# Layer norm rows on ScalarE, a layer norm's statistics six steps ahead, and one tile of the output projection in another step

## The chip, the core and the metric

The kernel runs on one core of a Trainium2 chip. Its engines work side by side: TensorE (PE, with its weight loads listed as PEld), VectorE (DVE), ScalarE (ACT), GpSimd (POOL) and SyncE (SP), which here only issues DMAs. The metric is the device time of one execution, in microseconds (us); a time given for a kernel is the median of its runs.

## The reference

The input has 16 elements of 512 rows by 128 (float32). For each element:

```python
h = layernorm(x) * (1 + ca) + sa
x = x + ga * attention(h)          # causal, 16 heads of 64, output projection W_out + b_out
h = layernorm(x) * (1 + cb) + sb
x = x + gb * moe(h)                # 8 experts 128 -> 512 -> 128, gelu, softmax over the top 2
```

The six modulation rows sa, ca, ga, sb, cb, gb are `silu(c) @ wmod`, one set for each element, and the two gates are kept at least 0.25 away from zero.

## The kernel before

**Attention, the first four fifths.** A loop runs over 128 pairs (b, n): element b from 0 to 15, and n from 0 to 7 for a pair of heads. One turn, by `attend`, is called a step here, and step n is the turn with that n. A step does, in PE's order: the scores of this pair (`scores`, L470, three banks for query tiles 3, 2 and 1+0), the product with V of the pair before (`z`, L558), the q and k projections of the next pair (`project_qk`, L426), the step's "units" (other PE work), and the transposes of this pair's probabilities (`transposes`, L530: tile 3, then 2, then 1 and 0).

The work between scores and transposes is a chain over four engines, once for each query tile: DVE takes the masked row maximum (`masked_max`, L487), ACT the exponentials (`exps`, L503), DVE a reciprocal of the row sum (`divide`, L510), POOL the division (L116, as all of POOL's operations that go through a helper). Then PE transposes, and the tile is copied to `pT`: tiles 3, 1 and 0 by DVE, tile 2 by ACT (L540). ACT also evicts z, q/k, v and hT.

All PSUM tiles come from one ring of four tiles of two banks. A tile can be written when the tile four places earlier has been evicted, so a late eviction holds up a matmul group later on.

**What sets the order.** PE, DVE, ACT and SP run exactly in program order, and POOL's operations are pinned to theirs. Other work is put into the steps by a table, `BESIDE`, and its variant `BESIDE_LAST` for element 15. Its slots are places in `attend`: `quiet` (a POOL scatter that waits for the first maximum), `a` (after the divide of tile 2), `b` (after that of tile 1), `units` (PE work, ahead of the transposes), `c` (ahead of the transposes and pT copies on DVE), `last` (behind them). A word `s.` stands for the next element's first layer norm and projections (`starting`), `f.` for the element before's output projection, residual, second layer norm and gate logits (`finishing`), `r.` for the routing two elements back, `1` for one scatter DMA of routed rows. The table before:

```python
0: dict(a="r.share", b="r.choose", quiet="1", units="f.o0 r.count", c="1 s.ln0 f.add0 r.rank", last="f.x0"),
1: dict(quiet="1", units="f.o1", c="1 s.ln1 r.extend r.place f.add1", last="s.dev f.x1"),
2: dict(b="s.norm0", quiet="1", units="v0", c="s.norm1 r.pick", last="rows"),
3: dict(units="s.hT", c="f.ln0"),
4: dict(quiet="1", units="v1", c="f.ln1 r.carry", last="f.dev"),
5: dict(a="f.off", quiet="1", units="s.v0", c="f.norm"),
6: dict(quiet="1", units="s.v1 f.hT", last="f.store"),
7: dict(units="f.lg", c="f.wt", last="m.mods"),
```

The names that matter:
- `ln0`, `ln1` (`layernorm`, L342, L343, L345): mean and variance of half an element's rows on DVE; `dev`: the power -0.5 on POOL; `norm0`, `norm1` (`normalise`, L354): (x - mean) * rstd on DVE, two row tiles each; `off` (`offset`, L389): -mean * rstd, used by the second layer norm, which POOL applies.
- `o0`, `o1` (`project_out`): two of the four row tiles of the output projection each; `add0`, `add1` (`projected`, L639): bias and eviction on DVE; `x0`, `x1` (`attended`): gate and residual on POOL.
- `extend`, `place`, `pick`, `carry`: parts of the routing on DVE, which give each routed row its slot; `pick` (L892 to L898) also takes the two expert weights.
- `lay_out`: fills DRAM, once, at the end of step 1 of element 0: `wall` (the experts' weights in rows, L274 to L284), `hs` (10 MB of empty rows, L288) and `ys` (L293). All go through SP's queue.
- `load_x` (L137): loads an element's rows, also on SP. It is issued at the start of step 0 of element b for element b + 1; only x_0 and x_1 are loaded at the start of the kernel.

**The experts, the last fifth.** The routed rows were scattered to slots in DRAM (`hs`); tiles of 256 rows go through one expert each (L1027 to L1065), are scattered back, and combined (`combine`, L1154 to L1163).

Of the kernel before, what the change touches and what calls it, by code (L numbers as in the profile page):

```python
# [9 lines left out]
FP = mybir.dt.float32  # L10
I32 = mybir.dt.int32
AF = mybir.ActivationFunctionType
# [3 lines left out]
P = 128  # L16
# [5 lines left out]
def kernel(  # L22
# [65 lines left out]
    def bank(name):  # L88
        return banks(name)[:, 0, :]
# [45 lines left out]
    def load_x(b):  # L135
        x = work.tile([P, NT, D], FP, tag="x", name=f"x_{b}", bufs=3)
        nc.sync.dma_start(out=x, in_=resid[b].rearrange("(t p) d -> p t d", p=P))  # L137
        x_tiles[b] = x
# [133 lines left out]

    def lay_out():
        nc.sync.dma_start(out=wall[:, :HID], in_=w1.rearrange("e d h -> (e d) h"))  # L274
        for k in range(NHC):
            nc.sync.dma_start(
                out=wall[:, HID + k * D : HID + (k + 1) * D].rearrange("(e p) d -> e p d", p=P),
                in_=w2[:, k * P : (k + 1) * P, :],
            )
        nc.sync.dma_start(  # L280
            out=wall[:, HID + NHC * D : HID + NHC * D + D].rearrange("(e p) d -> e p d", p=P),
            in_=b2.unsqueeze(1).to_broadcast([E, P, D]),
        )
        nc.sync.dma_start(  # L284
            out=wall[:, ROWW - NHC :].rearrange("(e p) k -> p e k", p=P),
            in_=b1T.rearrange("p (e k) -> p e k", k=NHC),
        )
        nc.sync.dma_start(  # L288
            out=hs.rearrange("(s p c) d -> p s (c d)", p=P, c=C),
            in_=empty.rearrange("p c d -> p (c d)").unsqueeze(1).to_broadcast([P, NST, C * (D + 1)]),  # L290
        )

        nc.sync.dma_start(  # L293
            out=ys[2 * LATE * S :, :].rearrange("(s p) d -> p s d", p=P),
            in_=empty[:, 0, :D].unsqueeze(1).to_broadcast([P, 2 * (B - LATE) * NT, D]),
        )
# [53 lines left out]

    def normalise(b, which, half_of):
        xn, mv, rstd = xn_tiles[b, which]
        for t in range(2 * half_of, 2 * half_of + 2):
            nc.vector.tensor_scalar(  # L354
                xn[:, t, :], x_tiles[b][:, t, :], mv[:, t, 0:1], rstd[:, t : t + 1], ALU.subtract, ALU.mult
            )
# [28 lines left out]

    def offset(b):
        _, mv, rstd = xn_tiles[b, 1]
        offs[b] = small.tile([P, NT], FP, tag="off", name=f"off_{b}", bufs=2)
        nc.vector.scalar_tensor_tensor(offs[b], mv[:, :, 0], -1.0, rstd, ALU.mult, ALU.mult)  # L389

    def second_norm(b):
# [3 lines left out]
        row = mods[b][:, 2 * D :]  # L395
        off = offs.pop(b)
        for t in range(NT):
# [149 lines left out]
    def z(b, n, ps=None):  # L547
# [6 lines left out]
        for t in reversed(range(NT)):  # L554
            for own in (True, False)[: NT - t]:
                cols = slice(t * P, (t + 1) * P) if own else slice((t + 1) * P, S)
                for j in range(2):
# [6 lines left out]
                    )  # L564
        zT = work.tile([P, S], FP, tag="zT", name=f"zT_{b}_{n}", bufs=NP + 2)
        zT_tiles[b, n] = zT
# [54 lines left out]

    def project_out(b, half_of):
        ps = bank(f"ps_o_{b}_{half_of}")
        attn_out[b, half_of] = ps
        for t in range(2 * half_of, 2 * half_of + 2):
            for n in range(NP):
                in_columns(
                    ps[:, ts(t % 2, D)],
                    zT_tiles[b, n][:, ts(t, P)],
                    wo_sb[:, n, :],  # L630
                    start=(n == 0),
                    stop=(n == NP - 1),
                )

    def projected(b, half_of):
        if half_of == 0:
            attn_sum[b] = work.tile([P, NT, D], FP, tag="o", name=f"o_{b}", bufs=1)
        ps = attn_out.pop((b, half_of))
        nc.vector.tensor_tensor(  # L639
            attn_sum[b][:, 2 * half_of : 2 * half_of + 2, :],  # L640
            ps[:, : 2 * D].rearrange("p (t d) -> p t d", d=D),
            bo_sb.unsqueeze(1).to_broadcast([P, 2, D]),
            ALU.add,
        )
# [88 lines left out]
    def starting(b):  # L733
# [5 lines left out]
            dev=(deviation, 0),  # L739
            norm0=(normalise, 0, 0),  # L740
            norm1=(normalise, 0, 1),
            hT=(first_hT,),
# [4 lines left out]
    def finishing(b):  # L747
# [4 lines left out]
            o0=(project_out, 0),  # L752
            o1=(project_out, 1),
            add0=(projected, 0),
            add1=(projected, 1),
            x0=(attended, 0),
            x1=(attended, 1),
            ln0=(layernorm, 1, 0),
            ln1=(layernorm, 1, 1),
            dev=(deviation, 1),  # L760
            off=(offset,),
            norm=(second_norm,),
# [36 lines left out]
    def route(b):  # L799
# [87 lines left out]
        def pick():  # L887
            wt, _ = chosen_by.pop(b)
            chosen = tiles["chosen"]
# [5 lines left out]
            slots_of[b] = tmp("slot", [P, 2, NT], I32, bufs=2)  # L895
            nc.vector.tensor_copy(slots_of[b], where)
            nc.vector.tensor_tensor(part, chosen, wt.unsqueeze(1).to_broadcast(both), ALU.mult)
            nc.vector.tensor_reduce(weight[:, :, at], part, AX.X, ALU.add)  # L898
# [9 lines left out]
        def experts():  # L908
# [23 lines left out]
        parts = dict(  # L932
            choose=choose, count=count, rank=rank, extend=extend, place=place, pick=pick, carry=carry_on
        )
# [204 lines left out]
    def fetch_x(b):  # L1139
        x2[b] = work.tile([P, NT, D], FP, tag="zT", name=f"x2_{b}", bufs=NP + 2)  # L1140
        nc.sync.dma_start(out=x2[b], in_=kept(x_rows[b]))
        load_gate_b(b)

    def combine(b, width=NT):

        x, got = x2.pop(b), got_tiles.pop(b)
        gb = gates_b.pop(b)
        y = work.tile([P, NT, D], FP, tag="zT", name=f"y_{b}", bufs=NP + 2)
        results[b] = y
# [97 lines left out]
    def dense_rest(b):  # L1247

        h = work.tile([P, NT, D], FP, tag="hT1", name=f"rest_h_{b}")
        nc.sync.dma_start(out=h, in_=kept(h2_rows[b]))  # L1250
        x = work.tile([P, NT, D], FP, tag="x", name=f"rest_x_{b}", bufs=3)
        load = nc.sync.dma_start(out=x, in_=in_rows(out[b]))
# [24 lines left out]
    warm_up(5)  # L1277
    begin["norm0"]()
    copied_scT()
    begin["norm1"]()  # L1280
    modulation()
# [5 lines left out]
    for task in later:  # L1287
# [4 lines left out]
    BESIDE = {  # L1292
        0: dict(a="r.share", b="r.choose", quiet="1", units="f.o0 r.count", c="1 s.ln0 f.add0 r.rank",
                last="f.x0"),
        1: dict(quiet="1", units="f.o1", c="1 s.ln1 r.extend r.place f.add1", last="s.dev f.x1"),
        2: dict(b="s.norm0", quiet="1", units="v0", c="s.norm1 r.pick", last="rows"),
        3: dict(units="s.hT", c="f.ln0"),
        4: dict(quiet="1", units="v1", c="f.ln1 r.carry", last="f.dev"),
        5: dict(a="f.off", quiet="1", units="s.v0", c="f.norm"),
        6: dict(quiet="1", units="s.v1 f.hT", last="f.store"),  # L1300
        7: dict(units="f.lg", c="f.wt", last="m.mods"),
    }

    BESIDE_LAST = {
        0: dict(a="r.share", b="r.choose", quiet="1", units="f.o0 r.count", c="1 f.add0 r.rank", last="f.x0"),
        1: dict(quiet="1", units="f.o1", c="1 r.extend r.place f.add1", last="f.x1"),
        2: dict(quiet="1", units="v0", c="r.pick", last="rows"),
        3: dict(quiet="1", units="v1", c="1 f.ln0 r.carry", last="r.experts"),
        4: dict(quiet="1", c="1 f.ln1", last="f.dev"),
        5: dict(a="f.off", quiet="1", c="1 f.norm"),  # L1310
        6: dict(quiet="1", units="f.hT", c="1", last="f.store"),
        7: dict(units="f.lg o01234", c="f.wt", late="o56", last="m.mods"),
    }

    FIRST = {
        0: dict(
            units=[begin["v0"], begin["v1"], modulation_matmuls],
            c=[modulation_rows],
            last=[lambda: later.pop()(), load_rest],
        ),  # L1320
        1: dict(units=[transposed_b1], c=[copied_b1], last=[lay_out]),
    }
    ends = finishing(LAST)
    for at, (b, n) in enumerate(pairs):
        prev = pairs[at - 1] if at else None
        nxt = pairs[at + 1] if at + 1 < len(pairs) else None
        if n == 0 and b + 1 < B and b + 1 not in x_tiles:
            load_x(b + 1)
        if n == 7 and b < LAST:
            routes[b - 1] = route(b - 1) if b else {}  # L1330
        known = {
            "s": starting(b + 1) if b + 1 < B else {},
            "f": finishing(b - 1) if b else {},
            "r": routes.get(b - 2, {}) | ({"share": finishing(b - 2)["share"]} if b > 1 else {}),
# [3 lines left out]
        for where, words in (BESIDE if b < LAST else BESIDE_LAST)[n].items():  # L1338
            for word in words.split():
# [8 lines left out]
                else:  # L1348
                    of, name = word.split(".")
                    tasks = [known[of][name]] if name in known[of] else []  # L1350
                beside.setdefault(where, []).extend(tasks)
        attend((b, n), prev, nxt, beside)

# [41 lines left out]
    steps = {at: [ends[name] for name in names] for at, names in steps.items()}  # L1395
    for at, name in enumerate(("share", "choose", "count", "rank", "extend", "place", "pick", "carry")):
        steps.setdefault(1 + at, []).append(routes[LATE][name])
# [95 lines left out]
```

## Time and profile before

| | us |
|---|---|
| median of the runs | 1549.77 (1549.37 to 1551.87, 3 runs) |
| the profiled execution | 1549.97 |
| its span, first to last instruction | 1548.2 |
| first scores matmul of element 0, 1, 2, 3 | 13.0, 86.3, 171.0, 248.6 |
| first scores matmul of element 6 and 7 | 481.93, 559.75 |
| first scores matmul of element 15, first expert matmul | 1182.6, 1269.7 |
| last PE instruction | 1528.2 |

The profile is of one execution. A line of a timeline has start and length in us, engine, source line, operation, output<-inputs, shape, count, and in brackets the idle time before it with what ended it. A line of the windows has a stretch, its length, and the busy time of PE, PEld, DVE, ACT and POOL in it (with counts), then PE's granted clock, the DMA share and GB/s. Each matmul and weight load stands twice in the counts, and a busy PE need not be PE at its best: a group that waits between two matmuls can show as one long busy piece.

### The profile page before, as it was taken

How to read it: one execution, taken by the hardware profiler on the slowest of the kernel's cores; microseconds unless marked ns; L12 is line 12 of the kernel's file. 1: busy time of each engine (PE TensorE's matmuls, PEld its weight loads, DVE VectorE, ACT ScalarE, POOL GpSimd, SP SyncE). 2: the span in 40 equal slices, each digit the busy share in tenths (PEclk: the TensorE clock that was granted, in tenths of full speed). 3: DMA queues.
4: the chain of work that ended last, by engine and by line, in shares of the span. 5: the costliest groups of instructions: out<-in, count | busy, mean ns of one | idle time of the engine just before them, and what ended most of it. 6: DMA issues, size and time to landing. Idle time of an engine off the chain costs nothing. (4 is left out here: it accounts for less than half of the span.)

```text
span 1548.2 us, 45464 instructions
## 1 busy us (share of the span) xinstructions
PE 1509.1 (97%) x16798; PEld 1048.2 (68%) x16798; DVE 1094.1 (71%) x4258; ACT 1062.6 (69%) x2887; POOL 966.7 (62%) x1561
## 2 busy tenths in 40 slices
PE   9989999999999999999999999999999999999994
PEld 5565757575756565656565656666666679999994
DVE  6657787878787878787878787878787844443444
ACT  6857777778777777777777777777777754444543
POOL 5435566666666666666666666666666656667663
PEclk9999999999999999999999999999999999999997
DMA  4860101010101010101010101010100047799994
GB/s 127 219 169 9 36 13 38 20 38 20 38 21 36 22 36 22 36 22 36 22 36 22 36 22 36 23 36 22 36 22 29 28 139 245 242 346 317 306 307 147
DMA packets 97902, 130.80 MB, mean 84 GB/s; under 512 B 10776, under 2 KB 73165, under 8 KB 97673
## 3 DMA queue, kind: packets, MB, share of 16 engines
q1 hardware_dynamic: 86745, 102.16, 21.5%
q0 software_dynamic: 10608, 24.73, 4.6%
q8 instruction: 136, 2.23, 0.6%
q14 instruction: 93, 0.76, 0.2%
q10 hardware_dynamic: 320, 0.93, 0.2%
HBM read 86.95 MB, written 46.07 MB: 86 GB/s over the span
## 5 line engine op out<-in xcount | busy, mean ns | idle before, releaser
L503 ACT ACTIVATE p<-p,nmax 128x512 f32<-128x512 f32 (+3 forms) x1024 | 560.3, 549 | 216.5 <-DVE nmax L487 214.9
L116 POOL TENSOR_SCALAR p<-p,rden 128x512 f32<-128x512 f32 (+3 forms) x1024 | 525.6, 529 | 230.0 <-DVE rden L510 225.0
L487 DVE CUSTOM_DVE_ANT_0 p<-sc,mask 128x512 f32<-128x512 f32 (+3 forms) x1024 | 439.9, 486 | 9.6 <-PE sc L470 9.0
L540 DVE COPY pT<-ps_pT 128x1024 f32<-128x1024 f32 (+2 forms) x384 | 276.6, 771 | 83.7 <-PE ps_pT L530 82.0
L470 PE MATMUL sc<-qk 64*128 64x512 f32 (+3 forms) x2048 | 311.0, 441 | 6.1 <-DVE o L639 4.4
L558 PE MATMUL ps_z<-pT,v 128*64 128x128 f32 x3556 | 304.0, 322 | 0.0
L116 POOL DMA_INDIRECT hs<-rows,slot x128 | 134.3, 1049 | 216.0 <-DVE nmax L487 144.8
L470 PEld LDWEIGHTS sc<-qk 64*128 64x128 f32 x2048 | 185.3, 189 | 117.0 <-DVE pT L540 55.8
L558 PEld LDWEIGHTS ps_z<-pT,v 128*64 128x64 f32 x3556 | 200.8, 137 | 33.7 <-issue 0.2
L530 PEld LDWEIGHTS ps_pT<-ident,p 64*128 64x128 f32 x5120 | 177.4, 139 | 62.9 <-POOL p L116 55.9
L530 PE MATMUL ps_pT<-ident,p 64*128 64x64 f32 x5120 | 201.3, 226 | 9.5 <-POOL p L116 6.6
L1043 ACT ACTIVATE hid<-ps_h,wexp 128x256 f32<-128x256 f32 x272 | 106.5, 474 | 127.9 <-issue 126.6
L503 ACT ACTIVATION_READ_ACCUMULATOR p<-p,nmax 128x1 f32 x1024 | 191.4, 187 | 0.0
L510 DVE RECIPROCAL rden<-den 128x2 f32<-128x2 f32 x512 | 84.0, 164 | 147.8 <-ACT p L503 143.2
L116 POOL DMA_INDIRECT ys<-yrow,to_rows x136 | 136.1, 1001 | 56.6 <-issue 31.0
L540 ACT COPY pT<-ps_pT 128x768 f32<-128x768 f32 x128 | 102.0, 797 | 98.6 <-PE ps_pT L530 95.9
L1056 PE MATMUL ps_e<-wexp,hid 128*128 128x128 f32 x1088 | 132.4, 275 | 0.0
L426 PE MATMUL ps_qk<-hT,wq_sb 128*64 128x512 f32 x508 | 130.6, 592 | 0.0
L426 PE MATMUL ps_qk<-hT,wk_sb 128*64 128x512 f32 x508 | 130.6, 592 | 0.0
L1041 PE MATMUL ps_h<-hsT,wexp 128*128 128x256 f32 x544 | 129.5, 381 | 0.9 <-DVE hsT L1029 0.9
L434 ACT COPY qk<-ps_qk 128x1024 f32<-128x1024 f32 x127 | 127.6, 1004 | 0.0
L1056 PEld LDWEIGHTS ps_e<-wexp,hid 128*128 128x128 f32 x1088 | 126.8, 192 | 0.1
(146 smaller groups left out, 1505.9 us busy)
## 6 DMA issues: line engine op xcount, KB each, us to landing
wexp<-wall SPq DMA_DIRECT2D x68, 578.0 KB
hs<-empty SPq DMA_DIRECT2D x1, 10062.0 KB
hrow<-hs SPq DMA_DIRECT2D x68, 129.0 KB
rows<-h_rows SPq DMA_DIRECT2D x32, 256.0 KB
got<-ys POOLq DMA_DIRECT2D x15, 512.0 KB, 6.3
x<-in_L_attn_resid_dram SPq DMA_DIRECT2D x16, 256.0 KB
mods<-mods_rows SPq DMA_DIRECT2D x16, 256.0 KB
x_rows<-x SPq DMA_DIRECT2D x16, 256.0 KB
```

The source lines that it names most:

```text
L116: made = getattr(nc.gpsimd, name)(*args, **kw)
L426: nc.tensor.matmul(out[r], lhsT[:, r], rhs, **flags)
L434: evictions.append(lambda: nc.scalar.copy(qk, ps))
L470: nc.tensor.matmul(ps[:, j, off : off + w], qk[r, 0, ts(i, P)], qk[r, 1, :w], start=True, stop=True)
L487: masked = nc.vector.tensor_tensor_reduce(out=p[:, j, r], in0=ps[:, j, r], in1=mask[:, S - (i + 1) * P : S], scale=-QSCALE, scalar=-MASKED ...
L503: nc.scalar.activation(p[:, j, r], p[:, j, r], AF.Exp, bias=nmax[:, j : j + 1], scale=-1.0, accum_out=den[:, j : j + 1])
L530: nc.tensor.transpose(ps[:, h, off + 2 * t + j, :], p[rows, j, at + t * P : at + (t + 1) * P], ident[rows, rows],)
L540: engine_copy(pT[:, : 2 * (i + 1), ts(i, P)].rearrange("p k (h q) -> p k h q", h=2), ps[:, :, off : off + 2 * (i + 1), :].rearrange("p h k ...
L558: nc.tensor.matmul(ps[j * DH : (j + 1) * DH, cols], v[:, t, col + j * DH : col + (j + 1) * DH], pT[:, t, j, cols], start=(t == NT - 1), st ...
L1041: nc.tensor.matmul(parts[j], wts[:, ts(j, P)], hT, start=True, stop=True)
L1043: nc.scalar.activation(hid[:, j, :], parts[j], AF.Gelu, bias=wts[:, ROWW - NHC + j : ROWW - NHC + j + 1])
L1056: nc.tensor.matmul(ps[:, ts(c, D)], hid[:, j, ts(c, P)], wts[:, HID + j * D : HID + (j + 1) * D], start=(j == 0), stop=(j == NHC - 1),)
```

## The change

It makes these edits:

- `normalise` goes from DVE to ACT: four `activation` calls an element (`Identity`, scale rstd, bias -mean * rstd), at the end of step 1 (`s.norm`). The bias comes from `offset`, which the first layer norm now uses too (`s.off` in step 0).
- The statistics (`t.ln0`, `t.ln1`, `t.dev`) of element b + 2 are taken in steps 5 and 6 of element b, where those of b + 1 were taken in steps 0 and 1. Element 1's are taken in element 0's first two steps as before. x has four buffers instead of three, and is loaded at the start of step 4 for element b + 2.
- `extend` and `place` move from slot `c` of step 1 to slot `b` of steps 1 and 2. The weights leave `pick` as a part of their own, `weigh`, in step 6.
- The output projection is cut in three: tiles 0 and 1 in step 0, tile 2 in step 1, tile 3 in step 3 (`o2`, `add2`); `x1` goes to step 3. zT has one more buffer (eleven).
- `lay_out` becomes a generator, `laid_out`: `hs` in six parts first, then `wall`, then `ys`; one part at the end of each step from step 1 of element 0 on.

The core of the diff:

```diff
-    def lay_out():
+    def laid_out():
+        n = NST // 6
+        for s in range(0, NST, n):
+            tiles = hs[s * TT : min(s + n, NST) * TT, :]
+            nc.sync.dma_start(out=tiles..., in_=empty...)
+            yield
         nc.sync.dma_start(out=wall[:, :HID], in_=w1.rearrange("e d h -> (e d) h"))
+        yield
...
-    def normalise(b, which, half_of):
-        xn, mv, rstd = xn_tiles[b, which]
-        for t in range(2 * half_of, 2 * half_of + 2):
-            nc.vector.tensor_scalar(
-                xn[:, t, :], x_tiles[b][:, t, :], mv[:, t, 0:1], rstd[:, t : t + 1], ALU.subtract, ALU.mult
+    def normalise(b):
+        xn, _, rstd = xn_tiles[b, 0]
+        off = offs.pop((b, 0))
+        for t in range(NT):
+            nc.scalar.activation(
+                xn[:, t, :], x_tiles[b][:, t, :], AF.Identity, bias=off[:, t : t + 1], scale=rstd[:, t : t + 1]
             )
...
+    OUT = ((0, 1), (2,), (3,))
...
-        0: dict(a="r.share", b="r.choose", quiet="1", units="f.o0 r.count", c="1 s.ln0 f.add0 r.rank",
-                last="f.x0"),
-        1: dict(quiet="1", units="f.o1", c="1 s.ln1 r.extend r.place f.add1", last="s.dev f.x1"),
-        2: dict(b="s.norm0", quiet="1", units="v0", c="s.norm1 r.pick", last="rows"),
-        3: dict(units="s.hT", c="f.ln0"),
+        0: dict(a="r.share s.off", b="r.choose", quiet="1", units="f.o0 r.count", c="1 f.add0 r.rank", last="f.x0"),
+        1: dict(b="r.extend", quiet="1", units="f.o1", c="1 f.add1", last="s.norm"),
+        2: dict(b="r.place", quiet="1", units="v0", c="r.pick", last="rows"),
+        3: dict(units="s.hT f.o2", c="f.add2 f.ln0", last="f.x1"),
         4: dict(quiet="1", units="v1", c="f.ln1 r.carry", last="f.dev"),
-        5: dict(a="f.off", quiet="1", units="s.v0", c="f.norm"),
-        6: dict(quiet="1", units="s.v1 f.hT", last="f.store"),
+        5: dict(a="f.off", quiet="1", units="s.v0", c="f.norm t.ln0"),
+        6: dict(quiet="1", units="s.v1 f.hT", c="r.weigh t.ln1", last="f.store t.dev"),
         7: dict(units="f.lg", c="f.wt", last="m.mods"),
...
+        3: dict(quiet="1", units="f.o2", c="1 f.add2 f.ln0 r.carry", last="f.x1 r.experts"),
+        4: dict(quiet="1", units="v1", c="1 f.ln1", last="f.dev"),
...
-        if n == 0 and b + 1 < B and b + 1 not in x_tiles:
-            load_x(b + 1)
+        if n == 4 and b + 2 < B:
+            load_x(b + 2)
...
+        if at:
+            beside.setdefault("last", []).append(lambda: next(laying, None))
```

The two lines for steps 3 and 4 of `BESIDE_LAST` took the place of `v1` with `f.ln0` in step 3 and no units in step 4. In the first element, `off` of element 1 stands at the end of step 1, behind POOL's power and ahead of `s.norm`.

## The prediction

> **What bounds the kernel now.** Read first: the page's engine line.
>
> ```profile
> PE 1509.1 (97%) x16798; PEld 1048.2 (68%) x16798; DVE 1094.1 (71%) x4258; ACT 1062.6 (69%) x2887; POOL 966.7 (62%) x1561
> ```
>
> TensorE (PE) is the bound, so what can be won is its 39 us of idle time and waits hidden inside busy groups. Next the windows cut at each step's first scores matmul, here steps 0 to 7 of element 6 (length, then busy us of PE, PEld, DVE, ACT, POOL, clock, DMA):
>
> ```profile
> 481.93:493.26 11.33, 11.33 (x166) 8.68 (x168) 9.77 (x40) 6.46 (x20) 7.14 (x13) 1.00 0.13 38
> 493.26:504.39 11.13, 11.13 (x162) 8.38 (x160) 9.24 (x40) 6.66 (x20) 8.47 (x13) 1.00 0.04 14
> 504.39:513.75 9.36, 9.36 (x108) 5.41 (x104) 8.30 (x33) 7.66 (x21) 6.13 (x11) 1.00 0.15 45
> 513.75:522.97 9.22, 8.74 (x106) 5.26 (x102) 7.65 (x28) 7.25 (x21) 4.17 (x9) 1.00 0.05 20
> 522.97:532.38 9.41, 9.41 (x103) 5.49 (x102) 7.58 (x33) 7.61 (x21) 6.00 (x10) 1.00 0.03 10
> 532.38:541.73 9.35, 9.35 (x106) 5.40 (x104) 6.52 (x25) 7.65 (x21) 6.32 (x13) 1.00 0.03 10
> 541.73:551.46 9.73, 9.73 (x115) 5.71 (x111) 6.15 (x24) 8.09 (x22) 8.41 (x13) 1.00 0.37 89
> 551.46:559.75 8.29, 8.29 (x115) 5.62 (x112) 6.68 (x31) 6.81 (x21) 4.11 (x8) 1.00 0.01 2
> ```
>
> Together 77.82 us; elements 3 to 14 repeat it (77.7 to 78.2). Only step 3 has a gap. Third, the PE timeline of step 3 (start, length):
>
> ```profile
> 513.75 2.65 PE L470 MATMUL sc<-qk 64*128 64x512 f32 x16
> 516.32 2.39 PE L558 MATMUL ps_z<-pT,v 128*64 128x128 f32 x28
> 518.54 1.03 PE L426 MATMUL ps_qk<-hT,wq_sb 128*64 128x512 f32 x4
> ...
> 520.66 0.66 PE L530 MATMUL ps_pT<-ident,p 64*128 64x64 f32 x16
> 521.48 0.59 PE L530 MATMUL ps_pT<-ident,p 64*128 64x64 f32 x12 [0.16 <-ACT zT L567]
> 522.39 0.59 PE L530 MATMUL ps_pT<-ident,p 64*128 64x64 f32 x12 [0.32 <-POOL p L116]
> 522.97 0.70 PE L470 MATMUL sc<-qk 64*128 64x512 f32 x2
> ```
>
> Step 1's groups, start to start: scores 2.31, ps_z 2.22, ps_qk 1.71, ps_o 3.60, ps_pT 1.29, all work. Step 3 needs 2.31 + 2.22 + 1.72 + 0.30 (ps_hT) + 1.29 = 7.84 and takes 9.22. Its scores take 2.57, because DVE in step 2 was busy with xn and pick until 9.17 and its pT copies, which free the banks, ended 0.33 later than elsewhere. Its transposes take 2.31: POOL's divides end at 8.62 and ACT frees the ps_hT bank at 9.17. So step 3 has room for 1.4 us of PE work, and step 1 none. Last, the one long wait, in step 1 of element 1:
>
> ```profile
> 98.20:116.00 17.80, 13.36 (x158) 9.64 (x158) 9.04 (x35) 6.07 (x19) 7.18 (x12) 0.81 0.12 34
> ```
> ```profile
> 102.46 0.29 DVE L342 BATCH_NORM_STATS2 st<-x 128x6 f32<-128x128 f32 x1 [9.49 <-DMA x<-in_L_attn_resid_dram]
> ```
> ```profile
> 103.77 2.93 PE L470 MATMUL sc<-qk 64*128 64x384 f32 x12 [4.44 <-DVE o L639]
> ```
>
> x_2's statistics stand on DVE ahead of the add of ps_o and the pT copies, and wait for a load issued at 97.98 behind the whole filling of DRAM.
>
> **Part 1, loads, filling and statistics.** The wait goes. Element 1's step 0 falls from 11.87 to 11.33 and step 1 from 17.79 to 11.13: 7.2 us (the gap of 5.0 and slower matmuls after it, clock 0.81). On SP, x_2 now follows three of six hs parts. The filling starts at 31.2; hs moved at about 290 GB/s (64 to 96 us), so 5.03 MB take 17 us and x_2 lands near 49. DVE asks for it in step 5 of element 0, near 66. Behind all six parts, the worst case, it would land near 67, a wait of 1 us. mods_0 lands near 67, asked for near 97. The wall copies took 27 us (31 to 58), so x_3 behind them lands near 97, asked for near 143. Later x loads follow the second rows load on SP, which goes out 6.6 into step 2; x is asked for in step 5. x_rows moves behind x1, to step 4; h_rows waits for step 6 anyway.
> The moved ln0 (0.80 from first start to the next operation) and ln1 (1.0 to 1.5) land in steps 5 and 6, where DVE sits 1.90 and 2.07 idle before the pT copy: 0, and with weigh (0.47) just covered in step 6; uncovered they cost up to 0.8. POOL's pow (1.04) goes to the end of step 6; POOL then idles 4.96 in step 7: 0.
>
> **Part 2, ScalarE normalises.** No row shows this instruction. The nearest is the combine's 128x128 Identity with one scale operand: four in 1.28 (timeline at 1342.31). The hT eviction with scale and bias takes 0.78 against 0.59 for the plain one, 0.09 for an operand, so four take 1.28 to 1.64; I take 1.64. They stand behind ACT's pT copy of step 1, which ends 0.69 into step 2; the exps, queued behind them, start at 2.25:
>
> ```profile
> 504.28 0.80 ACT L540 COPY pT<-ps_pT 128x768 f32<-128x768 f32 x1 [2.90 <-PE ps_pT L530]
> 506.64 0.72 ACT L503 ACTIVATE p<-p,nmax 128x512 f32<-128x512 f32 x1 [1.57 <-DVE nmax L487]
> ```
>
> The 1.57 gap covers all but 0.1, and the v copy at the end of the chain (9.19) has 0.17 to spare before the next scores: 0. In element 0 it isn't covered: `off` on DVE waits for POOL's pow (0.83 into step 2), ACT's four end near 3.6 instead of exps at 2.21; less 0.17, +1.1 once. At the start ACT's four replace DVE's 1.4 us, but ps_mod holds the transposes until 8.90: +0.1.
>
> **Part 3, routing.** Step 2's DVE loses xn (2.0) and weigh, gains place (0.72): its pT copy starts on time and step 3's scores return to 2.31. extend (1.45) and place now delay the last reciprocal. In step 1 it moves from 6.8 to about 7.6, POOL's last divide to 8.4, and its transposes stand near 9.1: 0. Beside POOL's divides DVE runs slower: in choose, nth took 0.53 against 0.20 in undisturbed elements and two 0.38 against 0.22, 0.5 in all; that still fits.
> The Trainium skill (SBUF — State Buffer, "SBUF: two separate sides") says a VectorE operation with two SBUF inputs and a GpSimd operation exclude each other for a whole instruction. By it each of extend's operations could wait out a divide, an estimate of 0.3 each and 0.7 us more per step 1, 10 in all; the choose row speaks for 0.
>
> **Part 4, the output's last tile.** Half of 3.60 leaves step 1: 11.13 to 9.33, -1.80. Step 3 becomes 7.84 + 1.80 = 9.64, +0.42: the transposes start at 8.35, the divides end at 8.13 (step 7's row, also without a scatter), ps_hT's bank is free at 8.8; nothing is waited for. But on DVE add2 waits for ps_o: 8.35 + 0.22 (step 0's lag) + 0.29 (a 128x256 add takes 0.43) - 0.08 overlap, then ln0 0.80: the pT copy starts at 9.58 against 9.09 (0.74 after the transposes begin). It ends 1.16 into step 4; ending at 1.02 gave scores of 2.57, so 2.72: step 4 +0.36. There DVE is late again with ln1 and carry: 0 to 0.35 in step 5, taken 0.15. x1 on POOL (1.46) ends some 0.8 into step 4, before its scatter at 3.1. The bank that o2 takes in the ring shifts the pT tiles to those of ps_z, ps_qk and ps_hT, free at 7.2, 8.1 and 8.8, each before PE comes to it. o2 holds the old element's eight zT tiles while three new ones are written; the eleventh buffer covers that, as the fourth x buffer covers the earlier load: 0 for both, and without them ScalarE's zT copy of step 3 would wait for o2.
>
> **Sum.** Elements 3 to 14: -1.80 + 0.42 + 0.36 + 0.15 = -0.87 each, -10.4. Element 2: its step 3 took 8.94, so -0.6. Element 1: -7.2 - 1.80 + 0.75 (step 3 from 8.89) + 0.36 = -7.9. Element 0: +1.2. Element 15: step 1 -1.8; v goes to step 4 behind add2, ln0, carry and experts on one DVE, 9.18 to about 11: 0. After attention PE is full (25.00 of 25 us) and one routing slot more hides: 0. Total -17.7: the profiled execution, 1549.97 (span 1548.2), becomes 1532.3; the median shown, 1549.77, is 0.2 lower: 1532.1.
>
> **Rivals.** (a) DVE's lateness after step 3 carries on through steps 4 to 6, at up to 0.87 an element, and the steps give nothing: only element 1's 7.2 less 1.2 remain, 1543.8. For it: DVE is busy 8.3 of 9.36 already in step 2. Against: 1.9 idle in steps 5 and 6. (b) Nothing is late and steps 4 and 5 keep their lengths: -1.38 an element, 7 us less in all, 1525. (c) Slower: ScalarE's normalising holds the exps of step 2. Every us beyond 1.73 (1.56 gap, 0.17 slack) counts 15 times; from 1.2 beyond, 0.73 an instruction, the kernel loses. The nearest row so dear is the 128x512 eviction, 0.78: four are 3.1, 15 x 1.4 = 21, less the gain: 1553. Against: 128 elements are a quarter of 512, and the 0.41 row. (d) x_2 still late, the reorder without effect: 1539; against it, the 17 us of cover.
>
> **How the numbers follow.** Forecast 0.62, (b) 0.16, (a) 0.14, (c) 0.05, (d) 0.03. The likeliest gives 1532.1. The range takes in (b) and most of the way to (a): 1525 to 1541. A measurement of this kernel tells 0.2%, 3.1 us, from no change: all but (c) end beyond that, with 0.02 for an (a) that costs more: 0.93 faster, 0.02 same, 0.05 slower.
>
> **What would show it.** Right: element 1's step 1 near 9.3 with no DMA behind DVE's statistics; steps 1, 3, 4 at 9.3, 9.6, 9.8; the gap in step 3 gone. Wrong: step 2 over 9.5 (part 2), step 1 over 9.6 with PE waiting for POOL (part 3), steps 4 to 6 together over 29.5 against 28.5 (a), a DMA wait in element 0's step 5 (part 1).

## The result, and the profile after

The changed kernel takes 1536.47 us (median of 4 runs, 1535.22 to 1537.13), the kernel before 1550.82 beside it (4 runs, 1549.37 to 1552.16): ratio 0.9903, 95% interval 0.9889 to 0.9918. It is faster, by 14.35 us. The forecast was 1532.1 with a range of 1525 to 1541. The profiled execution took 1536.24, with a span of 1534.5, 13.7 below the span before.

The page's engine line after:

```profile
PE 1505.1 (98%) x16798; PEld 1042.7 (68%) x16798; DVE 1089.1 (71%) x4225; ACT 1088.5 (71%) x2951; POOL 965.0 (63%) x1561
```

PE's idle time fell from 39 to 29 us, and PE's busy time by 4: the gain is part gaps, part waits inside groups. ACT took over the 26 us that the normalising costs it.

The windows of element 6's steps 0 to 7 after (stretch, length, busy us of PE, PEld, DVE, ACT, POOL, clock, DMA share, GB/s):

```profile
472.04:483.38 11.34, 11.34 (x167) 8.69 (x168) 9.23 (x37) 6.44 (x20) 7.06 (x12) 1.00 0.12 36
483.38:492.76 9.38, 9.38 (x130) 6.64 (x128) 7.93 (x31) 6.64 (x20) 6.30 (x12) 1.00 0.04 12
492.76:502.11 9.35, 9.35 (x106) 5.39 (x104) 8.03 (x31) 9.20 (x25) 5.87 (x10) 1.00 0.24 72
502.11:512.04 9.93, 9.93 (x138) 6.89 (x136) 6.62 (x29) 7.33 (x21) 4.82 (x9) 1.00 0.00 0
512.04:521.67 9.63, 9.62 (x106) 5.34 (x104) 8.08 (x33) 7.66 (x21) 6.47 (x12) 1.00 0.10 37
521.67:531.19 9.52, 9.52 (x106) 5.35 (x104) 7.40 (x29) 7.61 (x21) 6.61 (x13) 1.00 0.03 10
531.19:540.91 9.72, 9.72 (x114) 5.71 (x110) 7.62 (x31) 8.08 (x22) 9.35 (x14) 1.00 0.22 62
540.91:549.23 8.32, 8.32 (x115) 5.62 (x112) 6.71 (x31) 6.84 (x21) 4.27 (x9) 1.00 0.01 2
```

77.19 us instead of 77.82. Step 1 lost 1.75. Step 3 has no gap any more and grew by 0.71, steps 4 and 5 by 0.22 and 0.17; the others stayed. ACT's 9.20 busy us in step 2 did not make that step longer. By element, against the profile before:

| part of the span | predicted | measured |
|---|---|---|
| start and element 0 | +1.2 | +0.3 |
| element 1 | -7.9 | -7.87 |
| element 2 | -0.6 | -0.51 |
| elements 3 to 14 | -10.4 | -7.47 |
| element 15, steps 0 to 6 | 0 | +0.49 |
| element 15, step 7 | 0 | +0.60 |
| experts, to PE's last instruction | 0 | -0.34 |
| last stores | 0 | +1.08 |
| sum | -17.7 | -13.72 |

Element 1's step 1, the one long wait before, and the statistics of x_2, which now stand on DVE in element 0's step 5:

```profile
97.76:107.14 9.38, 9.38 (x130) 6.64 (x128) 6.34 (x25) 6.64 (x20) 4.87 (x10) 1.00 0.40 117
```
```profile
66.37 0.27 DVE L352 BATCH_NORM_STATS2 st<-x 128x6 f32<-128x128 f32 x1
```

9.38 after 17.80, at full clock, and no bracket behind the statistics: they wait for nothing. They come at 66.37, as reckoned ("near 66"). PE's timeline of step 3 after:

```profile
502.11 2.38 PE L482 MATMUL sc<-qk 64*128 64x512 f32 x16
504.42 2.39 PE L570 MATMUL ps_z<-pT,v 128*64 128x128 f32 x28
506.64 1.03 PE L438 MATMUL ps_qk<-hT,wq_sb 128*64 128x512 f32 x4
507.50 1.03 PE L438 MATMUL ps_qk<-hT,wk_sb 128*64 128x512 f32 x4
508.46 0.46 PE L379 MATMUL ps_hT<-ident,xn 64*128 64x64 f32 x8
508.85 1.97 PE L438 MATMUL ps_o<-wo_sb,zT 128*64 128x128 f32 x32
510.75 1.46 PE L542 MATMUL ps_pT<-ident,p 64*128 64x64 f32 x40
```

The transposes run through in one piece, where they had two gaps. Start to start, ps_qk takes 1.82 (506.64 to 508.46), ps_hT 0.39 and ps_o 1.90, each 0.1 more than the terms of the prediction (1.72, 0.30, 1.80). These are the places where groups whose PE tiles have 128 rows by 64 columns (`128*64`) meet groups of 64 by 128 (`64*128`). DVE at the end of the same step:

```profile
510.87 0.29 DVE L654 TENSOR_TENSOR o<-ps_o,bo_sb 128x128 f32<-128x128 f32 x1 [1.83 <-PE ps_o L438]
511.07 0.28 DVE L352 BATCH_NORM_STATS2 st<-x 128x6 f32<-128x128 f32 x1
...
511.89 2.12 DVE L552 COPY pT<-ps_pT 128x1024 f32<-128x1024 f32 x3
```

add2 stands 1.83 us on DVE waiting for ps_o with ln0 queued behind it. So the pT copy starts at 511.89, 1.14 after the transposes began instead of 0.74; step 4's scores take 2.59, step 5's 2.46, where 2.31 is the length without a wait.

### The profile page after: what moved, and what is told of

It is laid out like the page before. It is cut to its first block, busy times and chain, and to the rows that moved or that the text cites. A ratio compares the mean times of both kernels' runs of the same rounds, so it can differ in the third digit from the quotient of the medians.

```text
span 1534.5 us, 45505 instructions
## 1 busy us (share of the span) xinstructions
PE 1505.1 (98%) x16798; PEld 1042.7 (68%) x16798; DVE 1089.1 (71%) x4225; ACT 1088.5 (71%) x2951; POOL 965.0 (63%) x1561
## 4 chain that ended last, share of the span: by engine, by line
PE 94%; DVE 2%; ACT 1%; POOL 1%; issue 1%; DMA 1%; SPq 0%; POOLq 0%; DVEq 0%; ACTq 0%
PE ps_z L570 18%; PE sc L482 18%; PE ps_qk L438 13%; PE ps_pT L542 11%; PE ps_e L1084 8%; PE ps_h L1069 8%; PE ps_o L438 7%; PE ps_v L438 7%; PE ps_hs L1055 1%; ACT p L515 1%; POOL p L116 1%; PE ps_hT L379 1%; DVE pT L552 1%; PE ps_o_last L438 0%; PE ps_r L438 0%
## 5 line engine op out<-in xcount | busy, mean ns | idle before, releaser
L542 PEld LDWEIGHTS ps_pT<-ident,p 64*128 64x128 f32 x5120 | 173.8, 139 | 54.4 <-POOL p L116 45.0
L542 PE MATMUL ps_pT<-ident,p 64*128 64x64 f32 x5120 | 195.0, 226 | 2.6 <-POOL p L116 2.2
```

Of the source, the lines that this page charges most:

```text
L542: nc.tensor.transpose(ps[:, h, off + 2 * t + j, :], p[rows, j, at + t * P : at + (t + 1) * P], ident[rows, rows],)
```

## The experiments

Four runs were on each of three chips. On the first and the third the kernel before takes 1552.6 and 1552.4 us. On the second (e5 to e8) it takes 1571.4, the excess mostly in the experts' phase (first expert matmul to PE's last instruction: 282 us in e5, 259 in the profile before); the changed kernel was not run there. These four are read by their ratio to the kernel before on that chip, and by their steps.

### The terms of step 3: e1, e2, e3

Diffs against the changed kernel; e3 has both edits.

```diff
 e1
-        3: dict(units="s.hT f.o2", ...
+        3: dict(units="f.o2 s.hT", ...
 e2 (in the table of element 15 too)
-        3: dict(..., c="f.add2 f.ln0", ...
+        3: dict(..., c="f.ln0 f.add2", ...
```

e1:

> The changed kernel with one edit: in step 3 the units run in the order o2, hT instead of hT, o2. Theory 1 (PE pays about 0.1 us wherever a group of column-halved tiles, 128*64, meets one of row-halved tiles, 64*128): with o2 next to the q and k projections and hT next to the transposes, two of the four changes in step 3 go, step 3 falls from 9.93 to about 9.7. add2 finds ps_o about 0.4 earlier, so DVE's pT copy starts earlier and step 4's scores shorten by some 0.2. Together about -0.4 an element over elements 1 to 14, 5 us, 1531 in place of 1536.5. Rival (the 9.93 comes from evictions and the ring of banks, not from the order of groups): step 3 stays at 9.9, and hT, which now ends later, frees its bank later, 0 to +0.2 an element, 1536 to 1539.

Measured: 1529.36 (5 runs, 1527.45 to 1533.72), ratio 0.9848 (0.9834 to 0.9861). Step 3 takes 9.63 and step 4 9.38 in all of elements 1 to 14. PE's timeline of step 3 in e3, which has this order too:

```profile
504.94 1.03 PE L438 MATMUL ps_qk<-hT,wq_sb 128*64 128x512 f32 x4
505.80 1.03 PE L438 MATMUL ps_qk<-hT,wk_sb 128*64 128x512 f32 x4
506.65 1.92 PE L438 MATMUL ps_o<-wo_sb,zT 128*64 128x128 f32 x32
508.50 0.46 PE L379 MATMUL ps_hT<-ident,xn 64*128 64x64 f32 x8
508.80 1.41 PE L542 MATMUL ps_pT<-ident,p 64*128 64x64 f32 x40
```

The same matmuls: ps_qk now takes 1.71, ps_o 1.85, ps_hT 0.30. Between the scores and the transposes two changes of tiling are left instead of four, and the step is 0.30 shorter, 0.15 for each, where the theory had 0.1. Theory 1 holds: the order of the groups makes the 0.30 (e2 below changes the order of evictions alone and leaves step 3 at 9.92). Not shown is that the shape of the tiles is what costs it: here the `64*128` groups that moved are also the transposes. In the kernel before, ps_qk of step 3 starts at 518.54 and took 1.82 as well, up to its neighbour ps_hT:

```profile
520.36 0.46 PE L367 MATMUL ps_hT<-ident,xn 64*128 64x64 f32 x8
```

e2:

> The changed kernel with one edit: in step 3 DVE takes ln0 ahead of add2, in element 15 too, so that ln0 (0.80) no longer stands behind add2's wait for ps_o. Theory 2 (the lateness of steps 4 and 5 is DVE's wait for o2, as the prediction has it): the pT copy of step 3 starts near 9.1 instead of 9.77, step 4 falls from 9.63 to about 9.4 and step 5 from 9.51 to 9.35, -0.4 an element, 5 us, about 1531; step 3 stays at 9.93. Rival (steps 4 and 5 are long by their own DVE work, ln1 and carry): steps 4 and 5 keep 9.6 and 9.5, 1536.

Measured: 1530.58 (4 runs, 1530.42 to 1531.27), ratio 0.9861 (0.9846 to 0.9876). Step 3 stays at 9.92, step 4 is 9.36 and step 5 9.44. Theory 2 holds for step 4, and for nearly half of step 5's excess. Element 15's step 4 fell from 11.76 to 10.27.

e3:

> The changed kernel with both edits: units o2, hT and DVE's ln0 ahead of add2 in step 3. Theories 1 and 2 together: step 3 about 9.7, step 4 about 9.35, step 5 9.35: 76.7 instead of 77.2 an element, -0.6 over 14 elements, about 1528.5, faster than both kernels. Should theory 1 alone hold, 1531; should neither, 1536.

Measured: 1526.67 (5 runs, 1524.84 to 1529.55), ratio 0.9830 (0.9817 to 0.9844). Steps 3, 4 and 5 take 9.63, 9.36 and 9.45, as both theories say. But step 7 takes 8.76 to 9.00 in some elements and 8.32 in the others, in e1 too, and both profiled executions were the slowest of their five. DVE in step 6 of element 6 and of element 7, in e3:

```profile
535.75 1.48 DVE L918 TENSOR_TENSOR part<-chosen,wt 128x64 f32<-128x64 f32 x1
...
612.78 0.45 DVE L918 TENSOR_TENSOR part<-chosen,wt 128x64 f32<-128x64 f32 x1
```

This is the first operation of weigh. Of those in elements 3 to 13 (where ln1 follows it), six took 1.47 to 1.48 in e3 and eight 1.47 to 1.70 in e1: exactly the elements whose step 7 is long, by 0.45 or more each. In the changed kernel all 16 take 0.21 to 0.43. In the long case POOL is dividing in one run of eight operations:

```profile
533.66 4.15 POOL L116 TENSOR_SCALAR p<-p,rden 128x512 f32<-128x512 f32 x8
```

The prediction's row for such delays (choose) had at most 0.33 for one operation; here it is 1.03 beyond the short case. The Trainium skill (SBUF — State Buffer, "SBUF: two separate sides") says that a VectorE operation with two SBUF inputs and a GpSimd operation that reads SBUF lock each other out for whole instructions. The row agrees, and goes further: 1.03 is longer than any one of these eight divides, the longest of which take 0.68 (1.36 for two of 128x512). Taken one by one in the trace, the short multiply ends at 613.22, just after one divide (613.15); the long one ends at 537.23, after three divides have ended while it lasted (536.14, 536.59, 537.05). What decides between the two is open.

### The worth of the split: e4

```diff
-    OUT = ((0, 1), (2,), (3,))
+    OUT = ((0, 1), (2, 3))
...
-        3: dict(units="s.hT f.o2", c="f.add2 f.ln0", last="f.x1"),
+        3: dict(units="s.hT", c="f.ln0"),
...
```

> The changed kernel with part 4 undone: tiles 2 and 3 of the output projection both in step 1, x1 on POOL there too, no o2 and add2. Theory (by the terms measured in the changed kernel, the split gains 1.75 in step 1 and gives back most of it in steps 3 to 5): step 1 returns to about 11.13, steps 4 and 5 to 9.35, and step 3 to about 8.5, what element 0 takes without o2 now that step 2's DVE is no longer late (8.49): 11.13 + 8.5 + 9.35 + 9.35 = 38.3 against 38.45 now. So the split by itself is worth nothing, and this kernel lies within 3 us of 1536.5. Rival (the prediction's own reckoning: step 3 without the split stays near the 9.2 that it had): 39.0, +0.6 an element, 1545.

Measured: 1539.21 (5 runs, 1538.30 to 1540.23), ratio 0.9913 (0.9900 to 0.9927). Steps 1, 3, 4 and 5 take 11.13, 8.83, 9.40 and 9.35, together 0.25 more than in the changed kernel. Step 3 is 0.33 over the 8.5 expected, since a gap is left (PE's timeline of step 3):

```profile
511.88 0.46 PE L379 MATMUL ps_hT<-ident,xn 64*128 64x64 f32 x8
512.18 1.28 PE L542 MATMUL ps_pT<-ident,p 64*128 64x64 f32 x28
513.78 0.59 PE L542 MATMUL ps_pT<-ident,p 64*128 64x64 f32 x12 [0.32 <-POOL p L116]
```

By these steps the split as made is worth some 3.5 us (0.25 in 14 elements): the total lies within the 3 us expected, but it is not quite nothing, and the rival's 1545 did not come. The other parts alone bring step 3 from 9.22 to 8.83, before o's tile moves there.

### The load: e5, e12

e5 is the kernel before with one edit; e12 the changed kernel with another.

```diff
 e5
-        1: dict(units=[transposed_b1], c=[copied_b1], last=[lay_out]),
+        1: dict(units=[transposed_b1], c=[copied_b1], last=[lambda: load_x(2), lay_out]),
 e12
-        if at:
-            beside.setdefault("last", []).append(lambda: next(laying, None))
+        if at == 1:
+            beside.setdefault("last", []).append(lambda: [None for _ in laying])
```

e5:

> The kernel before with one edit: x_2 is loaded ahead of the filling of DRAM, at the end of step 1 of element 0; everything else as before. Theory (part 1 of the prediction: the wait in element 1 is the load behind the filling and nothing else): element 1's step 1 falls from 17.79 to 11.13 and its step 0 from 11.87 to about 11.33, 7.2 us, 1543.6 in a profile of 1550. Rival (the slow clock and the long steps of element 1 come with the filling's traffic, whatever x_2 does): steps 0 and 1 of element 1 keep part of their excess, 3 us or less are won.

Measured: ratio 0.9951 (0.9935 to 0.9968), 0.49% (the medians, 1564.94 and 1571.36, are 0.41% apart), where 7.2 us are 0.46%. Element 1's steps 0 and 1 take 11.13 and 11.14, the element 77.33 instead of 84.69. The wait was the load and nothing else, though hs was still being filled at 291 GB/s in the first of these steps:

```profile
86.82:97.95 11.13, 11.13 (x158) 8.39 (x160) 6.71 (x28) 6.33 (x20) 4.11 (x8) 1.00 1.07 291
```

e12:

> The changed kernel with the filling of DRAM issued at once, at the end of step 1 of element 0, hs first, then wall, then ys, instead of one part a step. x_2's load, issued in step 4, then stands behind all of it. Theory (the parts are what lets x_2 through; the queue moves 10 MB of hs and the wall in about 68 us from 31 on, so x_2 lands near 100, and the statistics that now ask for it in step 5 of element 0, near 66, stand on DVE ahead of that step's pT copy): element 0's step 5 or 6 takes some 30 us more, 1565 or more. Rival (putting hs ahead of wall is enough, or the queue takes several transfers at a time): x_2 comes in time, within 2 us of the changed kernel.

Measured: 1569.74 (2 runs), ratio 1.0113 (1.0095 to 1.0132), 34.7 us more than e9. DVE in element 0's step 5, ahead of that step's pT copy:

```profile
100.58 0.29 DVE L352 BATCH_NORM_STATS2 st<-x 128x6 f32<-128x128 f32 x1 [33.94 <-DMA x<-in_L_attn_resid_dram]
```

Step 6 takes 43.28 instead of 9.36. What the load waits for is SP: its issuing instructions for the filling last from 31.44 to 94.05, one after the other, and x_2's comes behind them, some 6 us before its rows are there:

```profile
92.17 1.88 SPq L303 DMA_DIRECT2D ys<-empty  x1
94.09 3.00 SPq L137 DMA_DIRECT2D x<-in_L_attn_resid_dram  x1
```

In the changed kernel it goes out at 39.00. With the load issued in step 4, as here, the early statistics are safe because the filling goes out in parts; with all of it issued at once the same code loses to the kernel before. A load ahead of the filling (e5) would be another way, not tried with the changed kernel.

### ScalarE's rows: e6, e7

e6 puts the two halves of the rows on DVE, as before, into slots b and c of step 2. e7 issues ScalarE's four instructions twice:

```diff
-        for t in range(NT):
+        for t in [*range(NT)] * (2 if b else 1):
```

e6:

> The changed kernel with part 2 undone for elements 1 to 15: the first layer norm's rows are normalised on VectorE again, two tiles in slot b of step 2 ahead of place and two in slot c ahead of pick; the rest stays, place in slot b too. Theory (DVE in step 2 has 0.24 to spare before its pT copy and gets 2.0 more, of which the wait for the last exponentials hides some): the last reciprocal comes 0.4 later and the pT copy of step 2 starts near 9.6 instead of 8.81, step 3 takes about 0.7 more, 10 us over the elements, 1546. Rival (the move to ScalarE did nothing, since DVE waits for PE anyway): within 2 us of 1536.5.

Measured: ratio 0.9989 (0.9975 to 1.0003). Step 3 takes 10.57 instead of 9.93, step 2 9.49 instead of 9.35: the pT copy of step 2 now starts 0.18 into step 3. The mechanism and step 3's 0.64 are as expected; with step 2's 0.14 that is 0.78 an element in elements 4 to 14, by these steps some 9 us in all for what the rows on ScalarE are worth. The total can't be set beside the 1536.5 of another chip; step 7 is 8.78 here too, where weigh's multiply takes 1.48, and step 1 is longer on this chip in e6 and e7 alike (9.48 and 9.57).

e7:

> The changed kernel with ScalarE's four normalising instructions of elements 1 to 15 issued twice (the same result written again): 3.3 us in place of 1.65 ahead of the exponentials of step 2. Theory (the cover is the 1.57 gap and 0.17 of slack at the v copy): 1.56 of it shows in each step 2, which goes from 9.35 to about 10.9, 15 times: 23 us, 1560, slower than the kernel before. Rival (step 2 has more room than the chain shows, since PE has 9.35 of other work): step 2 grows by 0.5 or less, 1544 or less.

Measured: ratio 1.0046 (1.0033 to 1.0059), slower than before. Step 2 takes 10.46, 1.11 more and not 1.56 (10.72 in element 6, which began this work 0.26 later). ACT in step 2 of element 6:

```profile
501.82 3.19 ACT L366 ACTIVATE xn<-x,off,rstd 128x128 f32<-128x128 f32 x8
504.91 0.71 ACT L515 ACTIVATE p<-p,nmax 128x512 f32<-128x512 f32 x1
```

The same place in the changed kernel, for comparison:

```profile
493.35 1.65 ACT L366 ACTIVATE xn<-x,off,rstd 128x128 f32<-128x128 f32 x4
495.02 0.72 ACT L515 ACTIVATE p<-p,nmax 128x512 f32<-128x512 f32 x1
```

Four take 1.65 (1.64 was taken), and the exponentials follow at once. Eight take 3.19 and show 1.11, so the cover is 2.08, not 1.73. Two things make the 0.35. The instructions overlap those before and behind them by 0.1 each, so that the exponentials start 1.42 later (3.67 into the step instead of 2.25) and not 3.19 - 1.57 = 1.62. And the chain behind them hides 0.31 of that, not 0.17. Where the cover is gone, the loss is real.

### The routing parts: e8, e9, e11

```diff
-        1: dict(b="r.extend", quiet="1", units="f.o1", c="1 f.add1", last="s.norm"),
-        2: dict(b="r.place", quiet="1", ...
+        1: dict(quiet="1", units="f.o1", c="1 r.extend r.place f.add1", last="s.norm"),
+        2: dict(quiet="1", ...
```

e8:

> The changed kernel with part 3 undone: extend and place in slot c of step 1, ahead of add1; weigh stays in step 6. Theory (with ln1 gone from step 1, DVE has 0.35 and 0.13 idle there, and the two together take about 2.1 from 6.9 on): the pT copy of step 1 starts about 0.2 late, step 2's scores grow by 0.1 or less, nothing else moves: within 2 us of 1536.5. Rival (the move out of step 1 was needed to make room): step 2 grows by 0.5 or more, 1543 or more.

Measured: ratio 0.9993 (0.9977 to 1.0010). Step 2 grew by 0.33, between theory and rival, and step 1 was 9.9. As step 1 was longer on this chip in every run, the kernel was run again beside the changed one.

e9:

> The changed kernel again, without an edit, as the yardstick for the three others on the same chip: ratio 0.990 to before, steps 1 to 5 of element 6 at 9.38, 9.35, 9.93, 9.63, 9.52 on a chip like the first. If the chip is like that of the runs e5 to e8 (before at 1571), step 1 at 9.5 and the expert phase some 24 us longer, with this kernel too.

Measured: 1535.06 (4 runs, 1534.66 to 1535.80), ratio 0.9891 (0.9876 to 0.9906). Element 6's steps are those of the first profile to 0.01. One step is not: element 15's step 7 takes 15.87 here and 17.30 in the first profile, with the same kernel. Its scores took 2.30 at a granted clock of 1.00 here, 3.73 at 0.61 there, and 3.14 at 0.73 in the kernel before.

e11:

> The kernel of e8 (extend and place in slot c of step 1) beside the changed kernel on the same chip. Theory, as e8 left it (extend and place take 2.6 and not 2.1 behind the last reciprocal, and step 1, shortened by the split of o, no longer covers them): steps 1 and 2 take 0.3 more each than with the routing moved, 8 us, ratio 0.995 to 0.996. Rival (e8's longer steps were that chip's): steps 1 and 2 at 9.38 and 9.4, ratio 0.990 as the changed kernel.

Measured: 1545.16 (5 runs, 1543.88 to 1545.42), ratio 0.9951 (0.9938 to 0.9965), 10.1 us over e9. Steps 1 and 2 take 9.65 and 9.68, 0.6 together over e9; up to the start of element 15 the two profiles differ by 8.6. DVE at the end of step 1:

```profile
492.67 0.17 DVE L522 RECIPROCAL rden<-den 128x2 f32<-128x2 f32 x1 [0.60 <-ACT p L515]
492.75 0.27 DVE L869 TENSOR_TENSOR lack<-upto,rooms 128x8 f32<-128x8 f32 x1
...
495.10 0.22 DVE L902 TENSOR_TENSOR upto<-upto,room 128x32 f32<-128x32 f32 x1
495.23 0.28 DVE L654 TENSOR_TENSOR o<-ps_o,bo_sb 128x128 f32<-128x128 f32 x1
495.42 2.14 DVE L552 COPY pT<-ps_pT 128x1024 f32<-128x1024 f32 x3
```

extend and place fill DVE from 492.75 to 495.32, add1 and the pT copy stand behind them, and the copy is 0.67 later in its step than in the changed kernel. e8's first theory had 2.1 for the two and expected next to nothing; it falls.

### A better version: e10

```diff
-        4: dict(quiet="1", units="v1", c="f.ln1 r.carry", last="f.dev"),
+        4: dict(a="r.carry", quiet="1", units="v1", c="f.ln1", last="f.dev"),
-        6: dict(quiet="1", units="s.v1 f.hT", c="r.weigh t.ln1", last="f.store t.dev"),
+        6: dict(a="r.weigh", quiet="1", units="s.v1 f.hT", c="t.ln1", last="f.store t.dev"),
 element 15, likewise, and
-        3: dict(..., last="f.x1 r.experts"),
+        3: dict(a="r.experts", ..., last="f.x1"),
```

The diff is against the kernel of e3.

> The kernel of e3 (o2 ahead of hT, ln0 ahead of add2) with carry, weigh and, in element 15, experts moved from slot c and the end of the step into slot a, the 0.8 that DVE waits between the second and the third reciprocal. There the chain has room: POOL takes up the divide of that tile only 1.2 after its reciprocal. Theory (carry makes the 0.1 of step 5; weigh's multiply, 0.44 by itself and 1.48 beside POOL's divides, makes the 0.45 of step 7 where that happens; experts and carry delay element 15): step 5 falls from 9.45 to 9.35, step 7 is 8.31 in every element, element 15's step 4 falls from 10.30 to about 9.4: -0.1 to -0.5 an element and -0.9, 3 to 6 us below e3, a ratio near 0.980. Rival (in slot a they hold up the third reciprocal and with it POOL): steps 4 and 6 grow by 0.3 or more, nothing is won.

Measured: 1524.26 (5 runs, 1524.04 to 1524.95), ratio 0.9821 (0.9808 to 0.9834): 10.8 us below the changed kernel beside it, 28 below the kernel before. Windows of element 6's steps 3 to 5 and 7:

```profile
498.97:508.60 9.63, 9.63 (x140) 6.88 (x136) 7.07 (x29) 7.42 (x21) 5.05 (x10) 1.00 0.00 0
508.60:517.95 9.35, 9.35 (x107) 5.39 (x104) 8.64 (x33) 7.66 (x21) 6.29 (x12) 1.00 0.11 38
517.95:527.30 9.35, 9.35 (x106) 5.42 (x104) 7.17 (x29) 7.65 (x21) 6.61 (x13) 1.00 0.03 10
...
537.03:545.34 8.31, 8.31 (x116) 5.62 (x112) 6.71 (x31) 6.83 (x21) 4.23 (x9) 1.00 0.01 2
```

An element takes 76.44, and element 15's step 4 9.35. weigh's multiply still takes 1.82 in two elements, but there the third reciprocal has 1.2 us of room, and step 7 stays at 8.31 or less in all of elements 1 to 14. In one place the rival's effect came: in element 2's step 4 carry's first operation took 1.83, the third reciprocal came 0.87 later than in the other elements, and the step takes 9.62. (weigh's multiply has 0.44 and 1.48 both beside POOL's divides; by itself, in the kernel before, it takes 0.22.) Over e3, medians differ by 2.4 us, less than the 3 to 6 expected, and the two ratios lie within each other's intervals; it is the steps that show the gain. The five runs of e10 lie within 0.9 us, those of e3 within 4.7.

## Why the prediction was right, and where it was off

- **Part 1** was right in every step: element 1 lost 7.87 for 7.9, x_2 was asked for at 66.37 and was there, and the moved statistics cost nothing in the changed kernel (e3 shows what weigh ahead of ln1 costs once it is uncovered, 0.45 in a step 7). e5 shows the wait alone to be worth 7.4 of element 1, e12 that the filling in parts is what keeps the early statistics from waiting.
- **Part 2**: 1.65 for 1.64, step 2 unchanged. Mis-sized was the cover, 1.73 for 2.08 (e7). In element 0 step 2 grew by 0.68 where 1.1 was reckoned; by its own terms the prediction should have had 3.6 - 2.21 - 0.17 = 1.22. ACT's four ended at 3.33 instead of 3.6, the exponentials started 1.03 late, and the chain hid 0.35 of that. Its step 3 lost 0.40 besides, because DVE no longer came late from step 2 (with the rows on DVE again, in e6, it is back at 8.89). Rival (c) was priced too high by the same cover; its kind of loss exists (e7).
- **Part 3**: "0" was right for the changed kernel. Beside the divides extend took 1.86 up to the next operation instead of 1.45, 0.4 more: near the 0.5 of the choose row and less than the 0.7 that the prediction estimated from the Trainium skill (SBUF — State Buffer, "SBUF: two separate sides"). PE never waited for it. What the prediction did not say is that this part has a price when left out: 10 us (e11). In e11 the parts left in slot c no longer fit the shorter step 1.
- **Part 4** holds the error. Step 1 lost 1.75 for 1.80. Step 3 was reckoned as 9.64 and took 9.93: the sum of groups took each group's length from a step with other neighbours, and o2 between hT and the transposes adds two changes of tiling. One of these lengths was misread: 1.72 is what ps_qk takes ahead of a group of its own tiling, and ahead of ps_hT it took 1.82 in the kernel before too (line under e1). The sum is thus that of the order o2, hT, and in that order e1 and e3 measure 9.63. Step 4 took 0.22 more for 0.36, step 5 0.17 for 0.15, by the mechanism named, add2 ahead of ln0 (e2; the other half of step 5's goes with carry, e10). Per element this is -0.62 for -0.87, 3 us over elements 3 to 14: most of the 4.0 missed. Of the -0.62 the split itself makes 0.25 (e4); the rest comes from the other parts, which shorten step 3 without it.
- **The rest**: element 15's step 4 took 11.76 where "about 11" was said (carry, experts and ln0 on one DVE, as named; e2 brings 10.27, e10 9.35). The 0.6 of its last step is no part of the change but the granted clock, which differs between executions of one kernel (e9). The 1.1 by which the last stores landed later was not foreseen. It stays in the other profiles of the changed layout (21.0 to 22.0 us behind PE's last instruction, against 20.0 in the kernel before and 20.2 in e5), and its cause is open. Some errors cancel: element 0 was reckoned 0.9 too dear, and step 4 too dear where step 3 was too cheap.
- **Rivals** (a), (b) and (d) did not come: steps 4 to 6 sum to 28.9, well under (a)'s 29.5; DVE was late, against (b); and x_2 was not, against (d). Most of (b)'s 1525 was to be had by two exchanges of order (e3; e10 moves three small parts more).

## What to carry to other kernels

When a group is put into a step that PE fills, price it with its neighbours: put it beside groups of the same tiling, and do not let the engine that evicts it wait for it with other work queued behind. Small work belongs where the chain it delays has room, not where its engine happens to be idle. A part that was reckoned at nothing was worth 10 us among the others, so each is to be tried by taking it out, not only by adding it.

## What the runs showed of the hardware

- In this kernel PE loses about 0.15 us where groups of `128*64` tiles and groups of `64*128` tiles follow each other: the same groups took 9.93 with four such changes and 9.63 with two (e1, e3). Whether the tiles or the kind of group makes it was not separated.
- A multiply of two SBUF operands on DVE (128x64), 0.22 in the kernel before, took 0.45 or 1.48 beside POOL's divides in one kernel (e3). Which of the two differs between elements of one execution, and each long one cost its element 0.45 us in e3 and nothing in e10.
- SP's issuing instruction can last nearly as long as the transfer ahead of it: in the kernel before, issuing the 1 MB of `ys` behind the 10 MB of `hs` (an estimate of 34 us at the 298 GB/s from 64 to 96) lasted 32.38 us, and x_2's load, next but one, went out at 97.98.
- The granted clock of one step differed between two executions of one kernel: 0.61 and 1.00 in the scores of element 15's step 7, 3.73 and 2.30 us.
- Chips differ by more than this change: the kernel before took 1552 on two and 1571 on one.
